# Merging each channel group with the image during the next group's attention, first scan rows from memory, half the query-key buffer

## The chip, the cores and the metric

The kernel runs on one core of a Trainium2 chip. A core has five engines with queues of their own: PE (matrix multiply; a matmul is a weight load, PEld, and a matmul proper), DVE (vector), ACT (scalar functions), POOL (a general engine) and SP, which here only issues transfers (DMA). They wait for one another through semaphores. [...] The metric is the device time of one execution, in microseconds (us); lower is better.

## The reference, cut to what matters

Input x has shape (2, 128, 128, 128): images n, channels, rows h, columns w. Four layers follow one another. The first is an axial attention along the rows of each image column, in 8 groups of 16 channels; its result is normalised, added to x and group-normalised:

```python
# after a group norm; one sequence per image and column, 8 channel groups
qr = einsum('bgci,cij->bgij', q, q_emb); kr = einsum('bgci,cij->bgij', k, k_emb).swapaxes(2, 3)
qk = einsum('bgci,bgcj->bgij', q, k)
sim = softmax(sum of the three, each batch-normalised, axis=3)
sv  = einsum('bgij,bgcj->bgci', sim, v)
sve = einsum('bgij,cij->bgci', sim, v_emb)
so  = batch_norm(concat([sv, sve]))          # statistics over all sequences, per channel
out = sum of the two halves per channel      # then x + out, then group norm (32 groups)
```

The second layer is four scans over the lines of the image (down, up, right, left). A line is the line's input plus `relu(conv1d(previous line))` with a 9-tap, 128x128-channel convolution. A deformable convolution and a 4x4 Hadamard convolution end the kernel; the change does not touch them.

## The kernel before, in words

**Prepare** (0 to about 390 us) builds q, k and v and writes them to scratch memory (qa, qb, v).

**Attention** (`layer0_attention`) runs 64 units: for each group g of 16 channels, each image n (2) and each block wc of 32 columns (4). A unit is 4 pairs of 2 x 4 columns, so the loop over m has 256 pairs and 8 more to drain the pipeline. Every engine issues in the order of the program (`InOrder`, line 81; all its instructions are recorded under line 83, so they are told apart by their tiles). In pair m PE turns the first half of the weights of pair m-3 (`turn`, tile te), transposes the position terms of pair m into lg, turns the second half (te again, one buffer), adds the query-key product from qk (`product_pe`), makes the position terms of the next unit (`terms_pe`, tile gen), and multiplies by v (`values`, tile po) and by the value embeddings (`embedded_pe`, po). DVE copies te to et (twice), inverts the sums (total), takes maxima (mx), adds the terms (e), scales part of gen (r), and in every second pair takes statistics of the sums (st_so). ACT makes the exponentials, the rest of r and the copy so. POOL divides (e<-e,total) and reorders et by position (`by_position`, et2, recorded as et<-et).

SP loads zz (from qb), vt (v; a tile 32 wide of which 16 are filled, the rest zero) and qk (a whole unit's query and key, two units in the buffer at partitions 0 and 64), and stores the sums sv and sve to scratch memory.

**Merge** (`Merge`) stands between attention and the scans. `begin` loads the first sums during the drain. `run` loads the image into res, computes scale and shift of all channels at once (`scales`), and for each of 8 units (n, wc) and half: ACT scales and transposes sv (u<-tv), DVE adds te (sve), DVE and POOL add the sum to res, DVE takes group-norm statistics (st_gn). The partitions are the 128 channels.

**Scans** (`layer1`): res is copied out to x1_d, and x1_d to x1c_d in blocks of 16 columns (for the last scan's residual). After `group_norm` the first scan (d = 0) normalises rows in place four ahead (`normalise`, ACT), runs 28 matmuls a line into pl, and DVE makes the new line (ln) from pl and the old row (`old`). POOL prepares the last layer's weights meanwhile (`prepare`).

Of the kernel before, what the change touches and what calls it, by code (L numbers as in the profile page):

```python
# [93 lines left out]
def layer0_prepare(env, x, prm, mem, alphas):  # L94
# [10 lines left out]
    with ExitStack() as ctx:  # L105
# [402 lines left out]
        with ExitStack() as part:  # L508
# [85 lines left out]
            for t in range(NT + 1):  # L594
                zs = positions(t) if t < NT else None
                if t >= wait:
                    share = -(-len(todo) // (NT + 1 - t))
                    for n, wc, b in todo[:share]:
# [11 lines left out]
                        if b == NB - 1:  # L610
                            halves = sa.rearrange("p (q r x) h -> p r q (x h)", r=2, x=RT)
                            for r in range(2):
                                nc.sync.dma_start(
                                    out=mem["qa"][:, n, wc, r].rearrange(
                                        "p (q x) h -> p q (x h)", x=RT
                                    ),
                                    in_=halves[:, r],
                                )
# [17 lines left out]
def layer0_attention(env, prm, mem, alphas, mv, then):  # L636
# [20 lines left out]
    with ExitStack() as ctx:  # L657
# [6 lines left out]
        sp = ctx.enter_context(tc.tile_pool(name="at_s", bufs=2))  # L664
        pp = ctx.enter_context(tc.tile_pool(name="at_ps", bufs=1, space=PSUM))
# [5 lines left out]
        vt = [cp.tile([P, WC, 32], F32, name=f"vt{j}", tag=f"vt{j}") for j in range(3)]  # L671
        for t in vt:
            nc.gpsimd.memset(t[:, :, 16:32], 0.0)
# [5 lines left out]
        qk = zp.tile([P, 2, HW, S], F32, name="qk", tag="qk")  # L679
# [3 lines left out]
        po_e = po.rearrange("p (i w) -> p i w", w=WC)  # L683

        qb = mem["qb"].rearrange("s (c t g) n e (i y) -> g n e i (s c) t y", c=8, t=2, i=4)
        qa = mem["qa"].rearrange("(c t g) n e r w h -> g n e r c t (w h)", c=8, t=2)
        sv = mem["sv"].rearrange("(g c) n e (q x) h -> g x c n e q h", g=NG, x=RT)
        sve = mem["sve"].rearrange("(g c) n e (s i) w -> g s c n e (i w)", g=NG, s=4)
# [6 lines left out]
        def load(at):  # L695
# [3 lines left out]
            u.base = 64 * (at % 2)  # L699
# [6 lines left out]
            sync.dma_start(out=u.v[:, :, 0:16], in_=mem["v"][u.g, u.n, u.wc])  # L706
# [3 lines left out]
        def load_qk(u):  # L710
            for r in range(2):
                lo = u.base + 32 * r
                sync.dma_start(
                    out=qk[lo : lo + 8].rearrange("p t w h -> p t (w h)"),
                    in_=qa[u.g, u.n, u.wc, r],
                )
# [31 lines left out]
        def position_pe(u, p):  # L748

            lg = pp.tile([P, 2, RT, S], F32, name="lg", tag="lg")  # L750
            for r in range(2):
                for x in range(RT):
                    pe.matmul(
                        lg[:, r, x, :],
                        lhsT=u.r[0][:, (2 * p + r) * RT + x, :],
# [8 lines left out]
        def product_pe(u, p, lg):  # L764

            for x in range(RT):
                for r in range(2):
                    lo = u.base + 32 * r
                    w = p * RT + x
# [9 lines left out]
        def add_term(u, p, lg):  # L779
            e = ep.tile([P, 2 * RT, S], F32, name="e", tag="e")  # L780
            dve.tensor_tensor(
                e,
                lg.rearrange("p r x j -> p (r x) j"),
                u.r[1][:, 2 * p * RT : 2 * (p + 1) * RT, :],
                ALU.add,
            )
            return e
# [34 lines left out]
        def by_position(u, p, et):  # L822
# [3 lines left out]
            lo = 2 * p * RT  # L826
            pool.tensor_copy(u.et[:, :, lo : lo + 2 * RT], et.rearrange("p w i -> p i w"))

        def values(u, p, et):

            for r in range(2):
                for x in range(RT):
                    pe.matmul(
                        po_v[32 * x : 32 * x + 32, r, :],
                        lhsT=u.v[:, (2 * p + r) * RT + x, :],
                        rhs=et[:, r * RT + x, :],
                        start=(r == 0),
                        stop=False,
# [3 lines left out]
        def embedded_pe(u, k, alone):  # L842

            for i in range(8 * k, 8 * k + 8):
                for s in range(4):
# [4 lines left out]
                        rhs=u.et[:, at, :],  # L850
                        start=(alone and i % 8 == 0),
                        stop=(i % 8 == 7),
# [3 lines left out]
        def both_copy(b, k):  # L856

            if k == 0:
                sos[b] = sp.tile([P, 4, 256], F32, name="so", tag="so")
            act.copy(sos[b][:, k, :], po)  # L860

        def store(b, so):
            for x in range(4):
                if b < len(units):
# [3 lines left out]
                        in_=so[32 * x : 32 * x + 16].rearrange("p k (r h) -> p (k r) h", r=2),  # L868
                    )
                if b > 0:  # L870
# [3 lines left out]
                        in_=so[32 * x + 16 : 32 * x + 32].rearrange("p k i -> p (k i)"),  # L874
                    )

        def stats(b, half):
            dve.bn_stats(
                st[:, b, half, :],
                sos[b].rearrange("p k i -> p (k i)")[:, 512 * half : 512 * half + 512],  # L880
            )
            per = N * NC
            for k in range(2):
                g, rest = divmod(b + 1 - k, per)
                if half == 1 and rest == 0 and g > 0:
                    g -= 1
                    every = st[:, per * g + k : per * g + k + per]
                    dve.bn_aggr(mv[:, g, k, :], every.rearrange("p e f k -> p (e f k)"))
# [6 lines left out]
        for at in range(2):  # L895
            us[at] = load(at)
            load_qk(us[at])
# [5 lines left out]
        for m in range(pairs + 8):  # L903
            here = m < pairs
            if m == pairs:
                early.close()
                then()
            u, p = us.get(m // 4), m % 4
# [9 lines left out]
            if here:  # L918
                lg = position_pe(u, p)
            if turning:  # L920
# [17 lines left out]
            if turning:  # L938
                values(ut, pt, et)
            piece = m - 7  # L940
            if 0 <= piece < pairs:
                embedded_pe(us[piece // 4], piece % 4, not turning)
            if m >= 3:
                both_copy((m - 3) // 4, (m - 3) % 4)

            for k, half in ((5, 0), (7, 1)):
                if m >= k and (m - k) % 4 == 0:
                    stats((m - k) // 4, half)
            if m % 4 == 3 and m // 4 + 2 < len(units):
                us[m // 4 + 2] = load(m // 4 + 2)  # L950
            if m >= 4 and m % 4 == 0 and m // 4 + 1 < len(units):
                load_qk(us[m // 4 + 1])
            if m % 4 == 3 and m >= 7:
                store((m - 7) // 4, sos.pop((m - 7) // 4))
            if m % 4 == 2 and m >= 14 and (m - 14) // 4 < len(units):
                us.pop((m - 14) // 4)

# [6 lines left out]
class Merge:  # L964
# [3 lines left out]
    def __init__(self, env, x, mem, ctx):  # L968
        self.env, self.x, self.mem, self.ctx = env, x, mem, ctx
        self.units = [(n, wc) for n in range(N) for wc in range(NC)]  # L970
        self.sums, self.embedded = {}, {}
        self.sync = InOrder(env.tc, env.nc.sync)

    def begin(self):
        self.sp = self.ctx.enter_context(
# [1292 lines left out]
```

## Time and profile before

| what | us |
|---|---|
| median of 3 runs (lowest, highest) | 5174.17 (5168.69, 5176.04) |
| the profiled execution, its span | 5167.96, 5166.2 |
| prepare | 0 to 390 |
| attention, with its drain | about 401 to 1808 |
| merge and group norm, to the first scan matmul | 1809.0 to 1949.7 |
| four scans | 1949.7 to about 3560 |
| the two convolutions | about 3560 to 5166 |
| busy, PE / DVE / ACT / POOL | 4861.6 / 3405.5 / 2721.3 / 2131.7 |

In the profile a line such as `1066.58 0.69 DVE L83 COPY et<-te ... [0.68 <-PE te L83]` says: at 1066.58 us from the start DVE ran a copy from te to et for 0.69 us; before it DVE stood idle for 0.68 us, until PE had written te. Busy is not the same as bound: an engine that is idle 12% of the time on average may have nothing left in one place of its loop.

### The profile page before, as it was taken

How to read it: one execution, taken by the hardware profiler on the slowest of the kernel's cores; microseconds unless marked ns; L12 is line 12 of the kernel's file. 1: busy time of each engine (PE TensorE's matmuls, PEld its weight loads, DVE VectorE, ACT ScalarE, POOL GpSimd, SP SyncE). 2: the span in 40 equal slices, each digit the busy share in tenths (PEclk: the TensorE clock that was granted, in tenths of full speed). 3: DMA queues.
4: the chain of work that ended last, by engine and by line, in shares of the span. 5: the costliest groups of instructions: out<-in, count | busy, mean ns of one | idle time of the engine just before them, and what ended most of it. 6: DMA issues, size and time to landing. Idle time of an engine off the chain costs nothing. (4 is left out here: it accounts for less than half of the span.)

```text
span 5166.2 us, 177668 instructions
## 1 busy us (share of the span) xinstructions
PE 4861.6 (94%) x76287; PEld 4289.0 (83%) x76287; DVE 3405.5 (66%) x6693; ACT 2721.3 (53%) x7723; POOL 2131.7 (41%) x1755
## 2 busy tenths in 40 slices
PE   7898999999999809999999999999989999999999
PEld 5767888888888708999999999997478888888877
DVE  3636888888888775555555555664456665666798
ACT  2567999999999755553224553222333343343222
POOL 3215777777777631000000002332045555555576
PEclk8998999999999959999999999999999999999999
DMA  3365444444444499900000000111311111111011
GB/s 157 125 239 91 65 65 65 65 65 66 65 64 67 106 369 188 90 25 2 1 2 1 1 1 18 36 48 53 124 45 33 33 34 39 34 34 32 36 50 58
DMA packets 753048, 347.61 MB, mean 67 GB/s; under 512 B 568836, under 2 KB 714884, under 8 KB 741504
## 3 DMA queue, kind: packets, MB, share of 16 engines
q1 hardware_dynamic: 746176, 326.48, 30.3%
q8 instruction: 604, 9.90, 0.8%
q10 hardware_dynamic: 6080, 9.69, 0.8%
q14 instruction: 188, 1.54, 0.1%
HBM read 195.12 MB, written 157.72 MB: 68 GB/s over the span
## 5 line engine op out<-in xcount | busy, mean ns | idle before, releaser
L83 PE MATMUL pl<-ln,wl 128*128 128x128 f32 (+1 forms) x10160 | 1228.7, 275 | 10.0 <-DVE ln L83 8.7
L83 PEld LDWEIGHTS pl<-ln,wl 128*128 128x128 f32 x10160 | 1177.2, 191 | 13.4 <-issue 6.2
L83 ACT ACTIVATE e<-e,mx 128x128 f32<-128x128 f32 x2048 | 793.7, 389 | 115.1 <-DVE mx L83 114.9
L83 POOL TENSOR_TENSOR w<-d 128x504 f32<-128x504 f32 x512 | 558.1, 1114 | 669.5 <-DVE s L83 485.8
L83 POOL TENSOR_TENSOR res<-ln,x1t 128x128 f32<-128x128 f32 x256 | 148.9, 582 | 1407.2 <-DVE ln L83 1394.4
L83 POOL TENSOR_TENSOR e<-e,total 128x1024 f32<-128x1024 f32 x256 | 485.4, 1896 | 390.2 <-DVE total L83 390.2
L83 ACT COPY res<-ln 128x64 f32<-128x64 f32 (+1 forms) x1016 | 284.0, 304 | 630.3 <-DVE ln L83 628.8
L83 ACT COPY sm<-ps_s 128x1152 f32<-128x1152 f32 x256 | 286.4, 1119 | 562.4 <-PE ps_s L83 562.4
L83 PE MATMUL po<-sm,wdef 128*128 128x256 f32 x2304 | 566.6, 391 | 0.0
L83 PEld LDWEIGHTS ps_s<-s,xw 28*128 28x128 f32 x10240 | 457.2, 187 | 121.0 <-issue 63.7
L83 PE MATMUL pl<-ln,ws 128*128 128x128 f32 x4064 | 537.3, 274 | 0.0
L83 PE MATMUL ps_s<-s,xw 28*128 28x240 f32 (+2 forms) x10240 | 521.0, 343 | 14.9 <-DMA xw<-px_d 12.3
L83 POOL COPY et<-et 128x1024 f32<-128x1024 f32 x256 | 529.2, 2067 | 1.1 <-DVE et L83 1.1
L83 DVE TENSOR_TENSOR v<-pl,c 128x128 f32<-128x128 f32 x508 | 148.2, 292 | 544.8 <-PE pl L83 540.0
L83 PEld LDWEIGHTS pl<-ln,ws 128*128 128x128 f32 x4064 | 495.2, 191 | 0.0
L83 PEld LDWEIGHTS po<-sm,wdef 128*128 128x128 f32 x2304 | 418.3, 190 | 70.3 <-issue 0.3
L83 DVE COPY et<-te 128x512 f32<-128x512 f32 x512 | 350.6, 685 | 118.8 <-PE te L83 107.1
L83 ACT ACTIVATE r<-gen,alphas 128x1536 f32<-128x1536 f32 x256 | 389.6, 1522 | 32.1 <-PE gen L83 32.1
L83 ACT ACTIVATION_READ_ACCUMULATOR e<-e,mx 128x1 f32 x2048 | 383.6, 187 | 0.0
L83 PE MATMUL gen<-zz,toep 32*128 32x128 f32 x8192 | 363.1, 281 | 15.2 <-DMA zz<-qb_d 10.9
L83 DVE STREAM_TRANSPOSE s<-w 128x1152 f32<-128x1152 f32 x256 | 349.9, 1367 | 32.3 <-PE ps_s L83 29.2
L83 DVE TENSOR_TENSOR e<-lg,r 128x1024 f32<-128x1024 f32 x256 | 313.5, 1225 | 58.4 <-PE lg L83 41.8
(253 smaller groups left out, 8461.1 us busy)
## 6 DMA issues: line engine op xcount, KB each, us to landing
xw<-px_d SPq DMA_DIRECT2D x528, 56.0 KB
xa<-in_x SPq DMA_DIRECT2D x16, 1024.0 KB
v_d<-vs SPq DMA_DIRECT2D x16, 1024.0 KB
qb_d<-sb SPq DMA_DIRECT2D x16, 1024.0 KB
qa_d<-sa SPq DMA_DIRECT2D x16, 1024.0 KB
zz<-qb_d SPq DMA_DIRECT2D x256, 64.0 KB
vt<-v_d SPq DMA_DIRECT2D x64, 256.0 KB
qk<-qa_d SPq DMA_DIRECT2D x128, 128.0 KB
```

The costliest lines, as they stand in the source:

```text
L83: return lambda *a, **k: self.tc.keep_in_program_order(issue(*a, **k))
```

## The change

The merge is no longer a stage for all channels at the end, but is done group by group. Once a group of 16 channels has been attended (32 pairs), its sums are merged with the image during the next group's pairs, one chunk in every four pairs. The partitions of a chunk are (image, block of columns, channel of the group), 8 x 16 = 128; a group has 8 chunks of 32 rows by 16 columns. In the loop, where m mod 4 is:

- 1: SP loads the chunk's te (sve), its xc (the image, laid out in blocks by the host as xm) and, for every fourth chunk, tv (sv);
- 3 (half a chunk's period later): POOL scales and shifts te;
- 0: DVE adds a times tv, read across its rows;
- 1: POOL adds the image;
- 2: DVE takes the statistics (st_x1) and SP stores the chunk to x1_d.

Scale and shift of the group come in four pairs before its first chunk: POOL squares, PE spreads them with two small matmuls into a te buffer, POOL takes the variance, DVE makes a first guess of the inverse root from the bits, and POOL refines it three times. The last group is merged after the loop (`last`), with ACT scaling in place of POOL.

The first scan reads its rows from x1_d in blocks of 16 rows (x1r, two buffers) and ACT writes its lines to res; res is no longer filled by the merge, and x1c_d is gone, as x1_d now has the blocked layout itself. `prepare` moves to the start of the second scan. qk holds one unit, loaded in halves of two pairs (`load_qk(nxt, p // 2)` after every second pair). vt is 16 wide and without zeros; PE does `embedded_pe` before `values`. qa, sv and sve have new layouts in memory; pair p now takes columns 4p to 4p+3 of both halves of the block.

```diff
 def layer0_attention(...)
+        merge.pool_in(ctx)
...
-        vt = [cp.tile([P, WC, 32], F32, ...) for j in range(3)]
-        for t in vt:
-            nc.gpsimd.memset(t[:, :, 16:32], 0.0)
+        vt = [cp.tile([P, WC, 16], F32, ...) for j in range(3)]
...
-        qk = zp.tile([P, 2, HW, S], F32, name="qk", tag="qk")
+        qk = zp.tile([P, 2, HW // 2, S], F32, name="qk", tag="qk")
...
-            sync.dma_start(out=u.v[:, :, 0:16], in_=mem["v"][u.g, u.n, u.wc])
+            sync.dma_start(out=u.v, in_=mem["v"][u.g, u.n, u.wc])
...
-        def load_qk(u):
+        def load_qk(u, half):
             for r in range(2):
-                lo = u.base + 32 * r
+                lo = 64 * half + 32 * r
...
-            pool.tensor_copy(u.et[:, :, lo : lo + 2 * RT], et.rearrange("p w i -> p i w"))
+            to = u.et.rearrange("p i (r w) -> p i r w", r=2)
+            pool.tensor_copy(
+                to[:, :, :, p * RT : (p + 1) * RT], et.rearrange("p (r x) i -> p i r x", r=2)
+            )
...
         for at in range(2):
             us[at] = load(at)
-            load_qk(us[at])
+        for half in range(2):
+            load_qk(us[0], half)
...
+            merge.before(m, lambda: pp.tile([P, RT, S], F32, name="te", tag="te"))
             if turning:
                 te = turn(e, 1)
...
+            merge.work(m)
             if m % 4 == 3 and m // 4 + 2 < len(units):
                 us[m // 4 + 2] = load(m // 4 + 2)
-            if m >= 4 and m % 4 == 0 and m // 4 + 1 < len(units):
-                load_qk(us[m // 4 + 1])
+            if p % 2 == 1 and nxt:
+                load_qk(nxt, p // 2)
             if m % 4 == 3 and m >= 7:
                 store((m - 7) // 4, sos.pop((m - 7) // 4))
+            merge.loads(m)
+        merge.last(lambda: pp.tile([P, RT, S], F32, name="te", tag="te"))
...
 class Merge:
+    def work(self, m):
+        g, k = self.step(m)
+        if g in range(NG - 1):
+            if k == 1:
+                self.squares(self.pool)
+            if k == 2:
+                self.variance(self.pool)
+            if k == 3:
+                self.first_root()
+                for _ in range(2):
+                    self.refine_root()
+            if k == 4:
+                self.refine_root()
+                self.scales(self.pool, g)
+        at = self.chunk(m, 3)
+        if at:
+            self.gather_stats(*at, self.te[at])
+            self.put(*at, self.te.pop(at))
+        at = self.chunk(m, 0)
+        if at:
+            te = self.te[at]
+            self.pool.tensor_scalar(te, te, self.a[:, 1:2], self.shift, ALU.mult, ALU.add)
+        at = self.chunk(m, 1)
+        if at:
+            self.add(self.te[at], self.tv, at[1] % 4)
+        at = self.chunk(m, 2)
+        if at:
+            te = self.te[at]
+            self.pool.tensor_tensor(te, te, self.xc.pop(at), ALU.add)
+    def add(self, te, tv, q):
+        self.dve.scalar_tensor_tensor(
+            te,
+            tv[:, :, 32 * q : 32 * q + 32].rearrange("p w h -> p h w"),
+            self.a[:, 0:1],
+            te,
+            ALU.mult,
+            ALU.add,
+        )
+    def refine_root(self):
+        y, v, t, pool = self.y, self.v, self.t, self.pool
+        pool.tensor_tensor(t, y, y, ALU.mult)
+        pool.tensor_tensor(t, t, v, ALU.mult)
+        pool.tensor_scalar(t, t, -0.5, 1.5, ALU.mult, ALU.add)
+        pool.tensor_tensor(y, y, t, ALU.mult)
+    def last(self, tile):
...
+        self.load_last(self.ltv, self.sv, 0, 8)
+        self.load_last(self.lte, self.sve, 0, 7)
+        self.load_last(self.lte, self.sve, 7, 8)
...
+        for i, (r, q) in enumerate(pieces):
+            te = part(self.lte, r, q)
+            self.act.activation(
+                te, te, AF.Identity, bias=self.shift, scale=self.a[:, 1:2]
+            )
+            self.add(te, self.ltv[:, r].rearrange("p (w h) -> p w h", h=S), q)
+            self.pool.tensor_tensor(te, te, part(self.lxc, r, q), ALU.add)
+            if i > 0:
+                finish(i - 1)
+        finish(7)
...
 def layer1(...)
-        for lo, hi in [(0, 4)] + [(h, h + 8) for h in range(4, S - 4, 8)] + [(S - 4, S)]:
-            for n in range(N):
-                nc.sync.dma_start(out=x1_d[:, n, lo:hi, :], in_=res[n][:, lo:hi, :])
...
+        rows = {0: load_rows(0, 4)}
...
         def normalise(h):
+            if h % CB == 0 and h + CB < S:
+                rows[h + CB] = load_rows(h + CB)
             for n in range(N):
                 act.activation(
-                    res[n][:, h, :],
-                    res[n][:, h, :],
+                    row(h, n),
+                    row(h, n),
...
+            if d == 1:
+                early.close()
+                prepare()
...
-                dve.scalar_tensor_tensor(new[0], v, 0.0, old[0], ALU.max, ALU.add)
+                dve.scalar_tensor_tensor(
+                    seen(new[0]), seen(v), 0.0, old[0], ALU.max, ALU.add
+                )
```

## The prediction

> **What bounds the kernel now.** I read the mean granted clock first (0.969, one core, nothing disturbed), then the page's 40 slices, then the busy time by stretch of time. The kernel has an attention stage (about 401 to 1808 us), a merge of its sums with the image (1808 to 1950) and four scans behind it. Busy time by stretch, columns as in the first line:
>
> ```profile
> core 0: us, PE busy (x) PEld busy (x) DVE busy (x) ACT busy (x) POOL busy (x), PEclk, DMA share, GB/s
> 430.00:1650.00 1220.00, 1203.06 (x32562) 1074.79 (x32562) 1071.87 (x1498) 1117.63 (x4122) 889.69 (x456) 0.99 0.44 65
> ...
> 1812.00:1840.00 28.00, 0.00 (x0) 0.00 (x0) 11.48 (x17) 11.68 (x7) 4.77 (x2) 0.50 0.98 401
> 1840.00:1945.00 105.00, 0.00 (x0) 0.00 (x0) 89.51 (x106) 54.66 (x27) 48.60 (x15) 0.50 0.88 351
> ...
> 2000.00:2300.00 300.00, 299.93 (x2685) 299.70 (x2684) 160.81 (x576) 164.09 (x671) 3.65 (x6) 1.00 1.12 71
> ```
>
> In attention PE is busy 99% of the time, so what delays PE there lengthens the kernel; DVE has 12% free, POOL 27%, ACT 8%. In the merge PE does nothing for some 140 us, and DVE (89.51 of 105 us) with the loads behind it sets the pace. In the scans PE is full again.
>
> Next, two neighbouring pairs of attention in order of time:
>
> ```profile
> 1065.16 0.74 DVE L83 TENSOR_SCALAR r<-gen,alphas 128x512 f32<-128x512 f32 x1
> ...
> 1065.82 0.66 PE L83 MATMUL te<-cst_main,e 128*128 128x128 f32 x4
> ...
> 1066.58 0.69 DVE L83 COPY et<-te 128x512 f32<-128x512 f32 x1 [0.68 <-PE te L83]
> ...
> 1067.32 0.42 PEld L83 LDWEIGHTS te<-cst_main,e 128*128 128x128 f32 x4 [0.22 <-DVE et L83]
> ...
> 1069.39 2.07 POOL L83 COPY et<-et 128x1024 f32<-128x1024 f32 x1
> ...
> 1070.98 0.68 DVE L83 BATCH_NORM_STATS2 st_so<-so 128x6 f32<-128x512 f32 x1
> ...
> 1071.79 0.69 DVE L83 COPY et<-te 128x512 f32<-128x512 f32 x1
> ...
> 1072.76 1.90 POOL L83 TENSOR_TENSOR e<-e,total 128x1024 f32<-128x1024 f32 x1 [1.31 <-DVE total L83]
> ```
>
> A pair takes 5.21 us (te at 1065.82, next at 1071.03). PE waits 0.22 us in every pair for the first copy of te. So that copy sits on PE's path: each microsecond that DVE comes late to it is a microsecond of the kernel. In pairs without statistics DVE is 0.68 us early, in those with them (1070.98) it arrives on time, with nothing left. POOL has 1.31 us free a pair.
>
> Last, the two ends of the stages:
>
> ```profile
> 414.66 1.66 PE L83 MATMUL lg<-cst_main,r 128*128 128x128 f32 x8
> ...
> 423.96 0.79 PE L83 MATMUL lg<-qk 8*128 8x128 f32 x2 [7.65 <-DMA qk<-qa_d]
> ```
>
> ```profile
> 1809.04 0.18 DVE L1012 TENSOR_TENSOR sq_out<-mv_out 128x16 f32<-128x16 f32 x1
> ...
> 1949.69 4.64 PE L83 MATMUL pl<-ln,wl 128*128 128x128 f32 x20 [3.67 <-DVE ln L83]
> ```
>
> The first shows PE held 7.65 us for qk as attention begins, the second the 140.65 us from the first step of the merge to the first scan matmul.
>
> **The change part by part.** The sum is made against the profiled execution (5167.96 us with a span of 5166.2), 6.2 us below the median of the runs shown (5174.17); differences are added to the median.
>
> *The separate merge goes; the last group stays (-95).* What is left between attention and scan: the last chunk's add and POOL sum (about 2.4 us) stand in the SP queue before the last loads, so these are issued near 1811.5; 2 MB at the 401 GB/s of the stretch above are 5 us, plus about 2 us until the first lands: data at 1819. Eight pieces follow, each an ACT pass, a DVE add, a POOL sum and DVE statistics (0.68). POOL needs 1.0 to 1.3 for 512 elements (its two-input groups of 504 took 1.11, the 512 of ws 1.27), the add 0.7 to 1.2 (below), and they get in each other's way, so 2.1 us a piece: 1819.5 + 8 x 2.1 + 1.2 = 1837.5. The row loads wait for the last store (about 2 us to land), then move 2,048 pieces of 256 B, some 6 us by the pace of the small pieces at 401 to 430 (154 GB/s); the group norm's chain (5.5 us, 1942.9 to 1948.4) runs beside that. Scan start near 1850 against 1949.7: -99. The next four rows land about 6 us behind, and ACT reaches them in the first step: +4. Ends: -85 with 3 us a piece, -107 with 1.2.
>
> *vt is loaded without gaps, qk in halves (-8).* vt was 4,096 pieces of 64 B ahead of qk in SP's queue, and qk's issue took 16.50 us (401.31). Now it is 128 pieces of 2 KB and only unit 0's qk is loaded first. PE still has the first position terms to do until 416.3; only the hold of 7.65 plus 0.32 goes. Bounds 0 and -10. In the steady state the halves come three pairs (15 us) ahead of use, as before about four; the DMA share (0.44) falls by vt's pieces and rises by 1 MB per four pairs: nothing, with 15 us of cover.
>
> *DVE's add into the chunk (+31).* One per chunk, 56 chunks, at the end of every fourth pair (one without statistics, 0.68 us early). Its contiguous price is 0.70 (half of te<-te,a_out,u, 1.277; 0.751 with PSUM). It reads tv across rows, 512 B apart. DVE's only rows of that kind are reductions: 66 elements in pairs of distant reads 0.225, 132 in fours 0.382, where its contiguous rows (mx 1.168 for 1024, mom 0.180 for 32) give 0.28; ACT's 512 strided (xc) took 1.107 against 0.586. So 0.70 to 1.25. It is also the first DVE instruction of attention that reads two SBUF tensors while POOL works. The trace shows such pairs collide: q<-dp took 0.676 to 2.055 (median 0.694), d<-o,base 1.307 where the least was 0.260, and POOL's res<-te,res 3.449 beside DVE against 2.406 alone. DVE is free at +5.16 of the pair, POOL's copy runs until +5.64, the copy of te is due at +5.97. Without a collision or stride: 5.16 + 0.70, no delay. With both: 5.64 + 1.2 - 0.07 = 6.77, 0.80 late. I take 0.55, the middle of the collided cases (0.30 and 0.80), because the collision rows are the nearest: 56 x 0.55 = 31; ends 0 and 45.
>
> [...]
>
> [...]
>
> *DVE's statistics of the chunk (0).* 0.68 us into the 0.68 us wait of the other free pairs; what hides it is the wait for te. If that is gone: 56 x 0.1.
>
> *The group's scales, seven times (+22).* Two small matmuls into te's buffer and a DVE copy stand between te's copy and its second half: no row has this; by the pieces about 0.75 (two waits like the 0.22 and a 0.16 copy). They wait for POOL's squares behind a delayed copy: 0.5. DVE's two root steps wait for POOL, whose copy ends at +0.43 of the next pair: 0.9. Then POOL does 16 tiny operations (nearest row: acc of 66 elements 0.314, of which 0.13 elements, so about 0.18 each) plus a chunk sum, 2 us more than its idle time: up to 1 us reaches te. Together 3.1 x 7 = 22; ends 10 and 35.
>
> *POOL's two passes per chunk (0).* 0.7 to 1.3 us into 1.31 us free, in different pairs; the product of POOL is due 1.6 us after it ends (1074.66 against te at 1076.27), which covers a first lateness.
>
> *Narrower values weights (0).* 16 columns instead of 32 in 16 loads a pair; 64 loads of 32 columns took 0.80 us, so at most 0.1 a pair: 0 to -26. I take 0, since the block's 0.64 us is nearest to its matmuls.
>
> *First scan from rows in memory (0).* Its DVE steps keep 128 elements (0.29) and about 0.35 us of slack under PE; each row block is issued some 12 steps of 3.13 us ahead. The weights for the last layer move from the first scan to the second: the same POOL work, nothing.
>
> Sum: -95 - 8 + 31 + 22 = -50, so 5174 - 50 = 5124 us.
>
> **The rivals.**
> *Attention pays nothing.* For it: POOL's copy has one source, and no row shows DVE held by such a copy; the tiny scale steps may all fall into idle time. Against it: 0.68 us is all the room there is. -95 - 8 + 10 = 5081, and 5055 if the narrower weights also tell.
> *DVE's add waits whole POOL instructions (slower).* If phases shift so that the add meets the start of a 2.07 us copy, as d<-o,base met a whole 1.07 us product, each costs 0.68 late becoming about 1.9. It decides from (103 - 22) / 56 = 1.45 us a chunk; at 1.9: 106 + 22 - 103 = +25, 5199. Against it: the copy is already 1.6 us old when DVE is free.
> *POOL becomes the bound (slower).* Its copy now writes runs of 4 instead of 8. If that cost what res<-ln,x1t cost (0.582 for 128, about 4 ns each), the copy takes 4.1 and POOL 6.0 of 5.2 us: 256 x 0.8 - 81 = +124, 5298. Against it: the reads, in the same order as before, look like the dear part (aqk 0.290 and wq 0.436 for 128).
> *The end stays long.* Pieces and row loads take 35 us more (the first scan waits on all stores): 5159.
>
> **How the numbers follow.** Forecast 0.60, its own range 5090 to 5160. Attention pays nothing 0.20, whole waits 0.08, POOL bound 0.07, long end 0.05. Leaving out POOL bound, half of whole waits and the lowest of the second case gives 5066 to 5188. Faster by over 0.2% (10 us, about what a measurement of this kernel tells from no change): 0.60 x 0.95 + 0.20 + 0.04 = 0.81; same 0.04; slower 0.15.
>
> **What would show it.** The wait of the first lg<-qk matmul gone; about 0.5 us more PE idle before the second te load in one pair of four; the add near 1.1 us and longer beside POOL; in seven places a pair longer by 2 to 3 us; from the last attention statistics to the first scan matmul about 40 us. The prediction is wrong if the pair's time grows in all pairs (POOL or DVE has become the bound), if no pair grows, or if the scan starts later than 60 us after attention.

## The result

The changed kernel takes 5201.46 us in the median of 4 runs (5197.45 to 5209.45), the kernel before 5174.3 us beside it (5168.69 to 5176.04). The ratio is 1.0056, with a 95% interval of 1.0039 to 1.0074: slower by 0.4 to 0.7%, where 50 us less had been forecast. The profiled execution of the changed kernel took 5202.09 us with a span of 5200.3, that of the kernel before 5167.96 with 5166.2. The clock is the same in both (0.966 and 0.969).

The busy time by stretch of the changed kernel, columns as in the first line: attention, two stretches of what is left of the merge, the first scan.

```profile
core 0: us, PE busy (x) PEld busy (x) DVE busy (x) ACT busy (x) POOL busy (x), PEclk, DMA share, GB/s
430.00:1650.00 1220.00, 1151.91 (x30744) 993.11 (x30740) 1089.74 (x1524) 1056.88 (x3888) 950.65 (x643) 0.97 0.40 99
1915.00:1945.00 30.00, 0.00 (x0) 0.00 (x0) 0.00 (x0) 0.00 (x0) 0.00 (x0) 0.50 0.46 120
1950.00:1970.00 20.00, 0.00 (x0) 0.00 (x0) 16.15 (x17) 4.50 (x7) 10.80 (x8) 0.50 0.36 102
2000.00:2300.00 300.00, 299.89 (x2685) 299.73 (x2684) 159.16 (x575) 164.60 (x672) 0.00 (x0) 1.00 0.13 43
```

PE's busy share of attention falls from 99 to 94%. In the second row nothing works but the DMA engines, at 120 GB/s and a share of 0.46. The merge of the kernel before ran at 401 GB/s and 0.98.

Which stretch of the span lost or gained is worked out from the starts of a few instructions: alphas, the first copy of te in each of the 256 pairs, the last aggregation of the attention statistics (mv_out), and the first scan matmul. The last three columns are runs told of below.

| us | before | after | e1 | e3 | e11 |
|---|---|---|---|---|---|
| start to alphas | 392.1 | 397.9 | 397.8 | 396.8 | 395.4 |
| alphas to the first copy of te | 47.2 | 44.5 | 46.3 | 44.8 | 36.6 |
| first to last pair (255 pairs) | 1353.4 | 1443.1 | 1392.1 | 1384.8 | 1387.6 |
| last pair to the last mv_out | 15.7 | 17.2 | 11.7 | 12.0 | 11.7 |
| mv_out to the first scan matmul | 141.3 | 78.4 | 48.2 | 48.3 | 38.5 |
| first scan matmul to the end | 3216.5 | 3219.2 | 3215.2 | 3214.2 | 3218.9 |

After minus before is 5.8 - 2.7 + 89.7 + 1.5 - 62.9 + 2.7 = +34.1 us. The first term lies in code that the change doesn't touch, and it comes and goes: in the sixteen profiled runs alphas starts between 389.9 and 399.5. So two things are to be explained: attention takes 90 us more, and the separate merge gave back 63 us and not 95.

**The end.** From the changed kernel's timeline:

```profile
1902.69 0.59 DVE L83 BATCH_NORM_AGGREGATE mv_out<-st_so 128x2 f32<-128x96 f32 x1
...
1909.57 0.61 SPq L83 DMA_DIRECT2D ltv<-sv_d  x1
...
1910.24 1.38 SPq L83 DMA_DIRECT2D lte<-sve_d  x2
...
1948.75 5.75 ACT L83 ACTIVATE lte<-lte,shift,a_out 128x512 f32<-128x512 f32 x8 [36.66 <-DMA lte<-sve_d]
...
1981.05 4.63 PE L83 MATMUL pl<-ln,wl 128*128 128x128 f32 x20 [5.04 <-DVE ln L83]
```

The loads are issued at 1909.57, as planned a few us after the statistics. ACT gets its data at 1948.75, 39.2 us later. The eight pieces behind take 2.16 us each, close to the 2.1 forecast.

**Attention.** Group 0, in whose time nothing is merged, takes 164.7 us (before: 165.4). Groups 1 to 6 take 182 to 185 us each where they took 169 to 175, and the 31 pairs counted of the last group 178 where they took 160. The mean length of a pair by its place in the group (groups 1 to 7, from the starts of the copies):

| place | 6 | 7 | 8 | 9 | 13 | 17 | 24 | 25 |
|---|---|---|---|---|---|---|---|---|
| before | 5.27 | 5.31 | 5.22 | 5.27 | 5.22 | 5.27 | 5.21 | 5.13 |
| after | 6.32 | 6.56 | 6.47 | 8.62 | 5.65 | 5.65 | 6.66 | 8.82 |
| e1 | 6.54 | 6.70 | 5.91 | 6.18 | 5.65 | 5.64 | 6.26 | 5.70 |

Places 13 and 17 stand for the pairs with nothing but an add: 0.44 longer than 5.21. Places 6 and 7 hold the scales: 2.46 longer together. Places 8, 9, 24 and 25 are the surprise, and they come one to three pairs behind the issue of tv. The profile of such a place, in order of time:

```profile
1286.42 0.62 SPq L83 DMA_DIRECT2D tv<-sv_d  x1
1287.10 0.60 SPq L83 DMA_DIRECT2D mte<-sve_d  x1
...
1287.75 0.61 SPq L83 DMA_DIRECT2D mxc<-in_xm  x1
...
1289.19 3.48 SPq L83 DMA_DIRECT2D zz<-qb_d  x4
...
1304.81 2.09 PE L83 MATMUL gen<-zz,toep 32*128 32x128 f32 x32 [4.35 <-DMA zz<-qb_d]
...
1306.89 0.75 DVE L83 TENSOR_SCALAR r<-gen,alphas 128x512 f32<-128x512 f32 x1 [4.99 <-PE gen L83]
...
1308.69 1.12 PE L83 MATMUL te<-cst_main,e 128*128 128x128 f32 x4
```

The first zz is issued 11.3 us before PE is ready for it (1304.81 less the hold of 4.35 is 1300.46), but 1.5 MB of the merge's loads were issued just ahead of it, and PE gets it 4.35 us too late. The hold costs more than itself: the four te matmuls behind it take 1.12 us where they take 0.66 in a quiet pair, and the granted clock is 0.70 in the stretch of another such place (930 to 941 us, 158 GB/s). Over attention the view of the waits says the same (engine, what it waited for, us in total, times, longest):

```profile
PE te L83 <- DVE et L83: 34.1, 67, 1.5
...
PE gen L83 <- DMA zz<-qb_d: 29.1, 10, 5.8
...
PE po L83 <- issue: 10.9, 4, 4.7
...
PE gen L83 <- issue: 7.0, 4, 3.4
```

The last three rows are 47 us. In the kernel before PE waits 9.8 us at po and 1.6 at gen with no releaser named, and none for zz.

Not every pair got longer. Over groups 1 to 6 the pairs at places 10, 14, 18, 22 and 23 took 5.74 us in the mean before the change, with single ones up to 8.1, and take 5.20 after it: 2.7 us less a group. In two of the long ones (at 893 and 1193 us) PE's hold, 1.8 and 2.3 us, is at po with no releaser named; what it waited for was not traced.

**The start.** The hold of PE for the first qk matmul, 7.65 us before:

```profile
427.06 0.79 PE L83 MATMUL lg<-qk 8*128 8x128 f32 x2 [5.17 <-DMA qk<-qa_d]
```

It is still 5.17. The queue's own waits between 398 and 440 us name the reason: SP couldn't issue qk until ve had landed, 1 MB in pieces of 64 B on ACT's queue.

```profile
SPq L83 <- DMA ve<-in_vemb: 13.8, 1, 13.8
```

### The profile page after: what moved, and what is told of

The parts are those of the page before. It is cut to its first block, busy times and chain, and to the rows that moved or that the text cites. A ratio compares the mean times of both kernels' runs of the same rounds, so it can differ in the third digit from the quotient of the medians.

```text
span 5200.3 us, 178400 instructions
## 1 busy us (share of the span) xinstructions
PE 4892.8 (94%) x76317; PEld 4273.0 (82%) x76317; DVE 3420.9 (66%) x6737; ACT 2662.6 (51%) x7703; POOL 2230.0 (43%) x2003
## 5 line engine op out<-in xcount | busy, mean ns | idle before, releaser
L83 PEld LDWEIGHTS ps_s<-s,xw 28*128 28x128 f32 x10240 | 456.9, 187 | 122.9 <-issue 78.4
L83 ACT ACTIVATE r<-gen,alphas 128x1536 f32<-128x1536 f32 x256 | 389.9, 1523 | 53.5 <-PE gen L83 53.5
L83 PE MATMUL te<-cst_main,e 128*128 128x128 f32 x2048 | 341.7, 290 | 41.4 <-DVE et L83 31.1
```

The costliest lines, as they stand in the source:

```text
L83: return lambda *a, **k: self.tc.keep_in_program_order(issue(*a, **k))
```

## The experiments

Theory A, formed from these traces: the merge's transfers are slow because of the order in which they walk memory (8 blocks outermost, 16 channels inside; the share of 0.46 in the second row above is that of 7.4 of the 16 DMA engines, and the theory takes it that the 8, or 7 in the larger load of lte, outermost set this number), and zz, behind them in SP's queue, comes late. Rival B: it is the place in the queue, the buffers or the sheer bytes, and order has nothing to do with it.

**e1: channels first.**

```
-            return t.rearrange("(g c) n e r h w -> g (n e) c r (h w)", g=NG)
+            return t.rearrange("(g c) n e r h w -> g c (n e) r (h w)", g=NG)
-        self.sv = mem["sv"].rearrange("(g c) n e (r w) h -> g (n e) c r (w h)", g=NG, r=2)
+        self.sv = mem["sv"].rearrange("(g c) n e (r w) h -> g c (n e) r (w h)", g=NG, r=2)
-        self.load_last(self.lte, self.sve, 0, 7)
-        self.load_last(self.lte, self.sve, 7, 8)
+        self.load_last(self.lte, self.sve)
```

> The changed kernel, but every load and store of the merge walks the 16 channels of a group first and the 8 blocks of the image second (before: 8 first, 7 in the last load of lte), and the last group's second operand is loaded in one piece; the constants follow that order. Same bytes, same pieces, same places in the queue. Theory A (a transfer whose outermost dimension is 8 or 7 runs on so many of the 16 DMA engines): the two last loads, 4 MB in 39 us at 124 GB/s with a DMA share of 0.48, take 10 to 14 us at a share above 0.9, so the stretch from the last group's attention statistics to the first scan matmul falls from 78 to about 50 us; tv lands in some 3 to 5 us and the waits for zz shrink to at least half (29 us of PE's time for gen now), together 45 to 70 us: 5130 to 5155 us. Rival B (the pieces, the memory rows or the queue order set the rate): the last loads stay near 39 us, and the time within 10 us of 5201.

Measured: 5107.21 us (5098.65 to 5113.14), a ratio to the kernel before of 0.9865 (0.9842 to 0.9888). The 4 MB land in 12.8 us; one row of e1's busy time by stretch, within that load:

```profile
1854.00:1864.00 10.00, 0.03 (x1) 0.00 (x0) 1.63 (x10) 0.20 (x1) 0.00 (x0) 0.50 0.96 395
```

The end shrinks from 78.4 to 48.2 us, attention by 51 us, and PE's waits for zz are gone from the list. SP's own waits between 600 and 1830 us, first the changed kernel:

```profile
SPq L83 <- DMA tv<-sv_d: 88.1, 13, 8.5
```

and then e1:

```profile
SPq L83 <- DMA tv<-sv_d: 6.2, 10, 1.1
```

So with the same bytes at the same places in the queue the whole loss goes, and more was gained (94 us of the medians) than Theory A had asked for (45 to 70). Rival B falls. With this order the change is worth 65 us, close to the 50 forecast.

**e2: zz ahead of the merge's loads.**

```
-            if m % 4 == 3 and m // 4 + 2 < len(units):
-                us[m // 4 + 2] = load(m // 4 + 2)
+            if m // 4 + 2 < len(units):
+                if m % 4 == 1:
+                    us[m // 4 + 2] = load(m // 4 + 2)
+                if m % 4 == 3:
+                    load_v(m // 4 + 2)
```

> The changed kernel, but the four loads of zz for the unit after next are issued in the second pair of a unit, ahead of the merge's loads, instead of in the fourth pair behind them; vt stays where it was. Theory A (zz is late because 1.5 MB of the merge's loads are in the same queue ahead of it): PE's wait for zz (29 us, ten times, up to 5.8) goes to under 5 us, the long pairs at places 8, 9, 24 and 25 of each group shrink from 6.5 to 13 us to at most 6, and the time falls by 35 to 55 us: 5146 to 5166. The last loads do not change (78 us to the first scan matmul). Rival B (SP is held by waits for buffers, and zz is only one of the things that come late): another wait, for tv, mte or POOL, takes its place, and no more than 15 us are gained: 5186 to 5201.

Measured: 5171.96 us (5156.11 to 5178.15), ratio 0.9991 (0.9978 to 1.0005). 29 us of the changed kernel's time are gained, less than the 35 that Theory A asked for at least and more than the 15 of Rival B. The waits for zz are gone, but a part came back elsewhere:

```profile
PE po L83 <- issue: 20.9, 8, 5.6
```

The matmuls of po, which need vt, now wait 10 us more than in the changed kernel, and vt is the load that stayed behind tv. (The profile names no releaser; that it is vt is inferred.) Here the slow loads made the next one in their queue late instead.

**e3: both edits.**

> Both edits of the two runs before this one. Theory A for both: the end gains 28 us as in the first, attention loses nothing more to zz: what is left is the strided add (56 x 0.45 = 25) and the scales (7 x 2.5 = 17) against the kernel before: 5174 - 95 + 30 (last loads as planned, so about 50 us instead of 20) + 42 = 5115 to 5135. If the first edit alone already ends the waits for zz, this run is the same as the first within 10 us.

Measured: 5106.71 us (5102.69 to 5110.0), ratio 0.9871 (0.985 to 0.9893), the same as e1, and below the 5115 to 5135 expected. With fast loads the place of zz no longer matters here.

**e4: the add reads tv as it lies.**

```
-            tv[:, :, 32 * q : 32 * q + 32].rearrange("p w h -> p h w"),
+            tv.rearrange("p w h -> p (w h)")[:, 512 * q : 512 * q + 512] ...
```

> The changed kernel, but the add into the chunk reads tv in the order in which it lies in memory, so it adds the wrong elements (the output is changed by that, the work is not). Theory A (the stride of 512 B sets the price of the add): the add takes 0.65 to 0.80 us instead of 1.21, and the pairs with it 5.20 to 5.30 instead of 5.65: some 20 to 25 us in sum. Rival B (it loses its time to POOL's copy beside it): the add gets no shorter than 1.0, or the pairs stay at 5.6.

Measured: 5190.41 us in one run. The view by tile gives the add's least, median and greatest duration in ns, first in the changed kernel:

```profile
L83 DVE SCALAR_TENSOR_TENSOR mte<-tv,a_out,mte x56: 1079/1218/2590, 667.0 to 1906.2; 128x512 f32<-128x512 f32 x56
```

and in e4:

```profile
L83 DVE SCALAR_TENSOR_TENSOR mte<-tv,a_out,mte x56: 740/926/1366, 668.1 to 1897.6; 128x512 f32<-128x512 f32 x56
```

The pairs with an add fall from 5.65 to 5.36. So of 0.44 us a chunk, 0.29 are the stride; 56 x 0.29 are 16 us, less than the 20 to 25 expected, and attention as a whole falls by 8 (1435.0). The add alone takes 0.74 (1.08 strided, as in the drain where POOL rests). Beside POOL's copy it takes 0.14 to 0.19 more in the median, and that is what is left of the copy when the add begins (0.35 to 0.43 us), less some 0.22. Where more is left, the add takes more, as at one place of the changed kernel:

```profile
1854.68 1.90 POOL L83 TENSOR_TENSOR e<-e,total 128x1024 f32<-128x1024 f32 x1
...
1854.83 2.59 DVE L83 SCALAR_TENSOR_TENSOR mte<-tv,a_out,mte 128x512 f32<-128x512 f32 x1
...
1856.52 2.68 POOL L83 COPY et<-et 128x1024 f32<-128x1024 f32 x1
```

POOL's product has 1.75 us to run when the add begins, and the add takes 1.51 us more than its 1.08; the copy that POOL begins before the add has ended takes 2.68 us where its mean is 2.06. Over the traces of the changed kernel and of the experiments, the 693 adds that begin with 0.3 to 2.0 us of a POOL instruction left take this remainder, less 0.18 to 0.27 us, longer than alone (1.08, and 0.74 in e4); the 106 that begin while POOL rests take at most 0.07 us longer. So the add waits for POOL's instruction. Both theories hold a part, the stride the larger.

**e5 and e6: the same bytes by block.** In e5 the last group's two loads, in e6 only tv, are issued as eight pieces of 16 partitions, one for each block.

> The changed kernel with its own order of partitions (16 channels of block 0, then of block 1, ...), but the last group's two loads are issued as eight pieces of 16 partitions each; the loads of the loop stay as they were. Theory A (the outermost dimension sets the number of DMA engines, and 16 partitions give 16): the 4 MB land in 11 to 16 us instead of 39, and the stretch from the last attention statistics to the first scan matmul falls from 78 to 50 to 56 us, with nothing changed in attention (1443 us between the first and the last copy of te, within 8): about 5175 us. Rival C (not the number of engines but the order of the partitions was cured by the first run): the loads stay above 30 us.

> The changed kernel, but only tv is loaded in eight pieces of 16 partitions; te, mxc and the store of the chunk stay on 8 engines, and so do the last loads. Theory A1 (tv, 1 MB twice a group, is what zz waits behind): SP's wait for tv (88 us) falls under 15, the long pairs at places 9 and 25 (8.6 and 8.8 us on the average) fall to 5.7 to 6.6, PE's wait for zz from 29 to under 10 us, and attention from 1443 to 1405 to 1420 us; the last loads still take 39 us: about 5170 us. Rival A2 (the three transfers of 256 KB in every chunk together do it): attention gains at most 12 us.

Measured: e5 5211.08 us. The 4 MB take 36.3 us, and the row of its busy time by stretch shows why the simple form of Theory A fails:

```profile
1920.00:1954.00 34.00, 0.34 (x2) 0.25 (x2) 1.63 (x10) 0.20 (x1) 0.00 (x0) 0.50 0.96 129
```

The share is 0.96, and yet 129 GB/s come in. The number of busy engines can't be the whole cause; Rival C's sign, more than 30 us, is what came. e6 took 5194.35 us; SP's wait for tv falls from 88 to 24 us and PE's for zz from 29 to 15, and attention takes 1430.5 us: 12.6 less. That is less than A1 and just beyond A2 (12 at most), and no more than noise may give: in e5, which leaves attention as it is, attention took 10 us more than in the changed kernel (1453.1). On how many engines the loop's other loads ran, no trace here shows.

**e7: scales for the first group only** (on e3).

> The kernel of the run with both edits, but the scales of a group are worked out for the first group only and used again for the six after it (so the output is changed; the statistics, chunks and loads are all there). By the trace of the run with both edits the pairs at places 6 and 7 of a group cost 6.96 and 6.41 us against 5.2: if the scales are the reason, both fall to 5.2 to 5.3 in groups 2 to 7 and attention gets 15 to 18 us shorter (1385 to about 1368). If loads or the chunk's passes are the reason, they stay above 6.

Measured: 5085.48 us. Places 6 and 7 go from 6.96 and 6.41 to 5.33 and 5.55 (that mean still holds the first group's scales), attention from 1384.8 to 1362.5. Without the scales these two pairs lose most of what they paid; the 22 us of the whole include some 6 at place 24, which changes from run to run.

**e8: ve behind qk.** The line that issues ve on ACT's queue was put behind the issue of qk in the program.

> The changed kernel, but ve (1 MB in pieces of 64 B, first needed seven pairs later) is loaded behind the first unit's qk and not ahead of it. Theory A (SP's issue of qk waits for the landing of ve, 13.8 us in the trace of the changed kernel): the hold of 5.17 us before the first lg<-qk matmul goes to under 1 us, and the first copy of te comes 40 us after alphas instead of 44.5. Rival B (qk waits for zz and vt of the second unit, which now stand ahead of it): the hold stays at 4 us or more.

Measured: 5204.27 us; the hold stays at 5.88. But the edit did not do what it was meant to: ACT's queue did not wait for SP's, and ve was issued at 408.95 and still first. SP waited 14.6 us for it. The run settles nothing; e11 does it better.

**e9, e10, e12: other shapes for the last loads** (on e1): two halves of 8 channels, eight pieces by block to every eighth partition, sixteen pieces by channel.

> The first run (channels first everywhere), but the last group's two loads are issued in two halves of 8 channels each, so the outermost dimension is 8 again, while every row of memory and every partition keeps the order of the first run. There the 4 MB landed in 12.5 us (395 GB/s at a share of 0.96). Theory K (the number of DMA engines alone set the slow rate): a share of 0.48 and 124 GB/s as in the changed kernel, about 35 to 39 us. Theory M (two things were mixed: half the engines, and an order of rows in which each engine is slow): a share of 0.48, but each engine as fast as in the first run (25 GB/s), so about 200 GB/s and 20 to 24 us. Theory O (only the order counts): 12 to 15 us.

> The first run, but the last group's two loads are issued as eight pieces by block of the image: 16 rows of memory each, as in the run that loaded by block (136 GB/s at a share above 0.9), only that the 16 rows now go to every eighth partition instead of to 16 neighbouring ones. Theory W (writes to 16 neighbouring partitions are what was slow there): 12 to 15 us for the 4 MB. Theory S (short transfers of one row for each engine, or the rows' distance of 128 KB in memory): 25 us or more, as there.

> The first run, but the last group's two loads are issued as sixteen pieces by channel: 8 rows of 16 KB that lie one behind the other in memory, to 8 neighbouring partitions, on 8 engines. [...] If neighbouring partitions written at the same time are what is slow: less than 110 GB/s, more than 38 us. [...]

Measured: the 4 MB take 23.1, 22.5 and 65.3 us from the first issue to ACT's first step (5118.19, 5116.58 and 5164.75 us in all). The busy time by stretch inside the load of e9:

```profile
1847.00:1867.00 20.00, 0.00 (x0) 0.00 (x0) 1.62 (x10) 0.20 (x1) 0.00 (x0) 0.50 0.96 201
```

of e10:

```profile
1846.00:1864.00 18.00, 0.00 (x0) 0.00 (x0) 0.97 (x6) 0.11 (x1) 0.00 (x0) 0.50 0.99 206
```

and of e12:

```profile
1846.00:1906.00 60.00, 0.00 (x0) 0.00 (x0) 1.01 (x7) 0.20 (x1) 0.00 (x0) 0.50 0.51 68
```

e9 came to the time that Theory M gave, but not for its reason: the share is 0.96 and not 0.48, at half of e1's rate (201 against 395 GB/s). e10 came out between its two theories: the same rows as in e5 take 22.5 and not 36.3 us when they go to every eighth partition instead of to neighbouring ones. e12 was the slowest of all: 65.3 us at 68 GB/s, as its case of neighbouring partitions has it (more than 38, less than 110). The pieces to 16 neighbouring partitions in e5 came at 129. But the changed kernel's loads don't do just that: their outer step is 16 partitions.

**e13: the loop's loads in halves** (on e1). It was meant as 8 engines; by e9 such halves came at a share of 0.96 and 201 GB/s, half of e1's rate, so the run says what half the rate costs in the loop, if the loop's halves are as slow as the last ones (not measured).

> The first run (channels first everywhere, last loads on 16 engines), but the loop's loads of tv, te and mxc are issued in two halves of 8 channels, so each runs on 8 engines again, in the order in which 8 engines reached 201 GB/s in the last loads. Theory K2 (in the loop it is the number of engines that made zz late): attention, 1392 us in the first run and 1443 in the changed kernel, comes out at 1425 us or more, and PE waits for zz by 15 us or more. Theory M2 (the slow order of rows and partitions did most of it): attention stays within 12 us of 1392, and PE waits for zz by less than 8 us.

Measured: 5126.3 us; attention takes 1406.8 us, 14.7 more than e1, and PE doesn't wait for zz. That is just beyond M2's 12 and far from K2's 1425. In this one run 15 of the 51 us come back.

**e14: the shapes one by one.** Seven loads of 2 MB ahead of the last ones, each waiting for the one before it.

> The first run, and ahead of the last group's loads seven more loads of 2 MB from the same tensor into the same tile, each waiting for the one before it, so that each one's rate stands alone (the tile is loaded anew by the right rows afterwards). A row is 16 KB. In order: 1, 128 rows as they lie; 2, the changed kernel's walk: outer dimension 8 with rows one apart, inner 16 with rows eight apart; 3, outer 8 with rows 17 apart, inner 16 rows one behind the other; 4, outer 16, rows 9 apart, inner 8 one behind the other; 5, outer 16 with rows one apart, inner 8 with rows sixteen apart; 6, two halves of 64 rows as they lie. Theory K (the outer dimension gives the number of engines and each engine keeps its 25 GB/s): 1, 4 and 5 take 5 to 6 us and some 2 us to land, 2 and 3 take 10 us and 2. Theory L (what slows an engine is that its rows are far apart, or that neighbouring engines read neighbouring rows): 2 and 5 are slow alike per engine (2: 17 to 19 us; 5: 9 us or more), 3 and 4 run at full speed per engine (10 and 5 us). Theory W (two engines that write into the same run of 8 partitions, or one engine into 16, slow each other): 3 is as slow as 2, 5 as fast as 1, and 6 takes twice as long as 1.

Measured (the kernel took 5197.65 us with these loads in it): from issue to issue 8.2, 22.0, 20.9, 12.5, 12.0 and 12.65 us. The busy time by stretch inside the six, in their order:

```profile
1847.00:1852.00 5.00, 0.94 (x4) 0.85 (x4) 1.64 (x10) 0.20 (x1) 0.00 (x0) 0.50 0.99 339
1858.00:1874.00 16.00, 0.00 (x0) 0.00 (x0) 0.00 (x0) 0.00 (x0) 0.00 (x0) 0.50 0.52 111
1879.00:1896.00 17.00, 0.00 (x0) 0.00 (x0) 0.00 (x0) 0.00 (x0) 0.00 (x0) 0.50 0.51 115
1898.50:1907.50 9.00, 0.00 (x0) 0.00 (x0) 0.00 (x0) 0.00 (x0) 0.00 (x0) 0.50 1.03 224
1911.00:1919.50 8.50, 0.00 (x0) 0.00 (x0) 0.00 (x0) 0.00 (x0) 0.00 (x0) 0.50 1.06 239
1923.00:1931.50 8.50, 0.00 (x0) 0.00 (x0) 0.00 (x0) 0.00 (x0) 0.00 (x0) 0.50 1.05 224
```

Rows 2 and 3 against 4 and 5: with an outermost dimension of 8 the share is 0.5 and the rate half (111 and 115 against 224 and 239 GB/s). How far apart the rows lie made no difference (2 is like 3, 111 and 115 GB/s; 5 like 4, 239 and 224), so Theory L falls. Row 1, 339 GB/s in the mean with its start, and the real load behind, 411 GB/s, are nearly twice as fast again: the form in which 128 rows go to 128 partitions as one plain list. Theory K lacks this second step, and Theory W is right on 3 and 6 and wrong on 5. So the changed kernel's walk comes at between a third and a quarter of the plain list's rate (111 to 115 against 339 to 411).

Whether the number of engines is a cause of it has not been shown: loads 2 to 5 change the share together with the partitions that the rows go to, and e5, at a share of 0.96, came at 129 GB/s, little more than these at half (111 to 120). A rival that no run tested alone is that the rate goes by where the rows land: pieces to 8 neighbouring partitions gave 68 GB/s (e12), to 16 neighbouring ones 129 (e5), to 16 that lie 8 apart 206 (e10), to 64 neighbouring ones 201 and 224 (e9, load 6). The changed kernel's load of ltv and loads 2 to 5 cover all 128 partitions each, and no trace here shows which of them are written at the same time, so whether the rival holds for these is not shown.

**e11: best of what was learnt.** e3, and ve issued by ACT behind the first unit's four position terms; the last loads in the order of the pieces; the weights of the scans 1 to 3 loaded during the first scan.

```
+        act.dma_start(out=ve[:, :, 16:32], in_=prm["vemb"])
...
+        for r in range(2):
+            self.sync.dma_start(out=self.ltv[:, r], in_=self.sv[NG - 1, :, :, r])
+            for q in range(4):
+                f = slice(512 * q, 512 * q + 512)
+                self.sync.dma_start(out=self.lte[:, r, f], in_=self.sve[NG - 1, :, :, r, f])
```

> Both edits (channels first, zz ahead of the merge's loads), and three more: ve is issued by ACT behind the first unit's four position terms; the last group is loaded in the order in which its pieces are worked on (one half of ltv, four pieces of lte, the other half, four pieces; the pieces of one half of the blocks first); the weights of the scans 1 to 3 are loaded during the first scan and not beside its first rows. By the traces: the hold for qk (5 us) goes to under 2, the first piece starts when 1.25 MB have landed and not 4 MB (6 us earlier), and the first rows land 2 to 3 us sooner. Against the run with both edits (5107) some 8 to 14 us: 5093 to 5099. If SP or the small pieces eat it up, it stays within 5 us of 5107.

Measured: 5097.48 us (5091.65 to 5104.45), ratio to the kernel before 0.986 (0.9844 to 0.9876): faster than the kernel before by 1.4%, and than the changed one by about 2%. The end is 38.5 us. The first qk matmul no longer waits:

```profile
419.66 1.09 PE L83 MATMUL lg<-qk 8*128 8x128 f32 x14
```

In e3, which differs in these first us only by the place of ve, that matmul is held 5.22 us and SP waits 14.1 for ve; here SP waits 0.2. That shows that ve held qk. Of the 8 us that the start gained against e3, 5.9 are lost again in group 0 (170.9 us against 165.0), where the first pair alone takes 9.63 us; what holds it was not traced further.

## Why the prediction was wrong

- **"2 MB at the 401 GB/s of the stretch above are 5 us, plus about 2 us until the first lands": the step that failed first.** ltv and lte are 2 MB each, so 4 MB and not 2, and they came at 120 GB/s. 39.2 us stand in the place of 7.5. In e1 the same 4 MB took 12.8, so of the 31.7 us missed some 5 are the bytes and 26 the rate. The rate was taken from loads that walk 128 channels outermost, and carried over to loads that walk 8 or 7 blocks outermost. With 8 or 7 outermost the DMA share was 0.46 here and 0.51 to 0.52 in e14 (8); the merge of the kernel before had 0.98. No run agrees with engine count as the only price: e5 had a share of 0.96 and 129 GB/s. The 2 us until the first lands are near what the kernel before shows for a small load: cst_main, 128 KB, was issued from 0.74 to 1.13 us and first read at 3.22. The term was -95; the two stretches behind the last pair gave -61.4.
- **"In the steady state ... nothing, with 15 us of cover": the step that failed worst.** It weighed the halves of qk and the DMA share, 0.44, and left out that the merge's own loads, up to 1.5 MB, stand in SP's queue ahead of zz, which has some 11 us and no more. 1.5 MB at the 158 GB/s of the stretch 930 to 941 are 10 us, an estimate, before zz itself moves. What is left of the pairs is 89.7 - 24.6 - 17.2 = 48 us, but that is net of a gain: by the table, the four places 8, 9, 24 and 25 cost 7 x (9.74 - 2 x 0.44) = 62 us, while places 10, 14, 18, 22 and 23 gave back 2.7 us a group, some 19, for which the sum had no term. e1 takes 46 of the 62 away, and 51 us over attention, by the order of rows alone.
- **The start (-8): mis-sized, -2.7.** The hold was put down to vt's 4,096 pieces alone. With them gone it only fell from 7.65 to 5.17: what holds qk in the changed kernel is ve on the other queue (13.8 us; e11), and qk had also been moved behind the second unit's zz and vt. In the kernel before SP's list shows no wait for ve, and how much of its hold was vt's is not shown.
- **DVE's add (+31): right.** 56 x 0.44 = 24.6. Two thirds are the stride: 0.74 without it and 1.08 with it (e4), inside the 0.70 to 1.25 that the prediction took from its rows. The rest is a collision like those in its rows: the add waits out POOL's instruction, less some 0.22 us. It cost little because the copy is nearly over by then: beside a copy that ran from 1005.26 to 1007.35 the add started at 1006.92 and took 1.30, its 1.08 and half of the 0.43 that were left. The rival of whole POOL instructions did come, but at one of the changed kernel's 56 adds (2.59 at 1854.83).
- **The scales (+22): right, 7 x 2.46 = 17.2** (places 6 and 7 against 5.21; e7).
- **The row loads' pace:** the prediction read 154 GB/s for 401 to 430 us; that stretch has 84. It was a small part of the -95.
- **At nothing, and rightly so:** the chunk's statistics and POOL's passes (pairs with these alone take 5.14 to 5.21), the narrower values weights (group 0 is 0.7 us shorter), the first scan. POOL's copy with runs of 4 takes 2.064 us as before (2.067), so that rival falls.
- **The rivals.** "The end stays long" had the right place and size, 38 us more than the 40 forecast, but alone it gives 5159; the loss in attention was in none of them. The prediction named the sign to look for, a scan that starts later than 60 us after attention (78).

With the order of rows mended (e1), the total comes into the range, 5107 against 5124, but partly by luck. The two stretches behind the last pair give -97 for the -95 and the start -1 for the -8. Attention gives +39 for the +53, though it still loses some 16 us at places 8, 9, 24 and 25, because of the 19 us gained that nobody had counted.

## What to carry to other kernels

Before a load's rate is taken from another load, compare the patterns: what stands outermost, and whether it is one plain list of 128 rows to 128 partitions; here the same bytes took 12.8 or 39.2 us. Which of the two things in the pattern counts, the number of engines at work or the partitions that the rows go to, is open. When transfers are added to a queue, list what is issued behind them, and compare its time to use with the landing of everything ahead of it, not with the mean DMA share: a mean share of 0.40 hid some 60 us of loss. Look at the other queues too: ve, on ACT's, held SP's issue of qk for 13.8 us.

## What the runs showed of the hardware

- A high DMA share was not a high rate. At a share of 0.96 to 1.05, loads of sv and sve came at 129 (e5), 201 (e9), 224 (e14) and 395 GB/s (e1), by the form of the transfer. Rows sent to 8 neighbouring partitions came at 68 GB/s and a share of 0.51 (e12).
- Between an outermost dimension of 16 with an inner one of 8 (224 to 239 GB/s, e14) and 128 plain rows (395 in e1, 411 in e14) lies a factor of nearly 2, and another between 16 and 8 outermost (111 and 115, e14). What they come from is not settled here.
- SP's issue of qk waited 13.8 us for the landing of ve, a load of ACT's queue (the changed kernel).
- DVE's add of 512 elements took 0.74 us when both sources lie in order (e4) and 1.08 when one is read 512 B apart (the changed kernel).
- DVE's add of tv into a chunk waited for POOL's running instruction: with 0.3 to 2.0 us of it left, 693 adds took that remainder, less 0.18 to 0.27 us, longer than alone. POOL waited too: a copy that began under such an add took 2.68 us and not 2.06.
